# A four-layer graph network on one core: FFN chunks of 4, 4, 4, 4, 4, 3, 2, 1 blocks instead of 3, 4, 4, 4, 4, 4, 2, 1, and the last block's V work in one go

## The chip, the cores and the metric

The kernel runs on one core of a Trainium2 chip. The metric is the device time of one execution in microseconds (us), the median of three runs. Before the change it is 2567.61 us (2564.39 to 2570.67).

## The reference

There are 3327 nodes with 256 features and a sparse 0/1 adjacency matrix. Layer 0 is a simple graph attention over the neighbours. Layers 1 to 3 are transformer layers whose attention is masked by the same adjacency; each of them computes

```
q, k, v = split(layer_norm(x) @ w_qkv)          # 8 heads of 32
attn    = softmax(where(adj != 0, q·k * SCALE, -inf))
x       = x + (attn · v) @ w_proj + b_proj
x       = x + gelu(layer_norm(x) @ w1 + b1) @ w2 + b2     # 256 -> 1024 -> 256
```

About 16 of the 3327 entries of an adjacency row are set, so attention is a weighted sum over a short list of neighbours.

## The kernel before, in words

Layer 0 reads the whole adjacency matrix, makes a list of neighbours for each node and sorts the nodes by degree into 26 blocks of 128 (`NB`). Block 0 holds the nodes with most neighbours: `CAPS` says how many list entries each block has, from 40 for block 0 and 24 for block 1 down to 10 for block 25. The K and V rows of all nodes lie in a DRAM table `kv[L]`, one for each of the layers 1 to 3.

Layers 1 to 3 go through the blocks in the hand-written `ORDER` 25, 1, 24, 2, 23, 3, ... 10, 15, 11, 14, 12, 13, 0 (L1268): long and short ones take turns, and the longest, block 0, comes last. The lists are cut into groups of at most four entries (`slots`, L1275): 121 groups in a layer, ten of them for block 0. `issue` (L1288) fetches a group: for each of its entries GpSimd (POOL) starts one indirect DMA that brings 128 rows of K and V, 2 KB each, into one of the ten buffers (`NBUF`) of a ring. A buffer is free for the next group when the V work of its group is done.

`run` (L1556) writes the order of everything by hand; each engine executes its own instructions in that order. One turn of its inner loop takes one group g of block b:

- `scores` (here called K work): VectorE (DVE) multiplies K by q (L1325) and sums over the head dimension (L1326); after the last group `softmax` follows (L1331, exp on ScalarE, ACT).
- `value`, called once or twice in a turn (L1577), takes the oldest group of an earlier block whose scores are done (`todo`): `values` (V work) multiplies V by the weights on DVE (L1366), sums over entries by transposing matmuls on TensorE (PE, L1372), and issues the next group of gathers (L1375). In a turn of block 0 it is always called twice.
- `some` (L1544) emits pieces of what comes later. `short` holds the five steps of a finished block (`block`: copy, projection on PE, residual add on DVE, L1400). `long` holds the steps of an FFN chunk. Each turn adds `rate` to a credit, and steps with a cost in a made-up unit are taken from `long` while the credit is above zero.

An FFN chunk is made of several finished blocks[...]. When the last block of a chunk has had its residual add, `chunk` (L1411) appends its steps to `long`: normalisation (`scale2`, `turn`, `hT`), eight `up` and eight `down` matmul pairs with a GELU on ACT between them (L1439, L1445, L1462), the way back to rows (`shift`, `back`), the residual adds, and, in layers 1 and 2, the normalisation, Q, K, V (L1492) of the next layer and the store of the new K and V rows (`keep`, L1498 to L1500). In layer 3 the output rows are stored by POOL instead (`store`, L1505). All of a chunk's steps depend on each other in a row across DVE, ACT and PE.

The next layer's gathers may touch any row, so they begin only when the last chunk's K and V rows have been stored: between two layers POOL has nothing to do.

What the change touches:

- the sizes of the chunks (L1270): 3, 4, 4, 4, 4, 4, 2, 1, in the order of `ORDER`. The last ones are 10, 15, 11, 14 (here C10/4, called by its first block and its size), 12, 13 (C12/2) and 0 (C0/1); the one before is C8/4.
- the pace (L1405 to L1407): the sum of the costs in `long`, divided by the number of groups of the next four blocks less two, and by five for the chunk that ends with block 13.
- how often `value` is called (L1577), and the loop after the last group (L1583), in which each `value` is followed by `some`, so that FFN steps are mixed into the V work of block 0.

Of the kernel before, what the change touches and what calls it, by code (L numbers as in the profile page):

```python
# [32 lines left out]
NB = (N + P - 1) // P  # L33
# [25 lines left out]
NBUF = 10  # L59

CB = 4
# [447 lines left out]
@with_exitstack  # L509
def kernel(ctx: ExitStack, tc: tile.TileContext, ins, out: bass.AP):  # L510
    nc = tc.nc
    keep = ctx.enter_context(tc.tile_pool(name="s_keep", bufs=1))
    dram = ctx.enter_context(tc.tile_pool(name="s_dram", bufs=1, space=DRAM))
    flag = keep.tile([1, 1], I32, name="flag")
    E = mybir.EngineType
    with tc.manual_schedule(engines={E.PE, E.DVE, E.Activation, E.Pool, E.SP}):
        with ExitStack() as inner:
            sparse_path(inner, tc, ins, out, dram, flag)
    unfit = nc.values_load(flag[0:1, 0:1])
    with tc.If(unfit > 0):  # L520
        general_path(tc, ins, out)


def sparse_path(ctx, tc, ins, out, dram, flag):
# [98 lines left out]
    with tc.tile_pool(name="a", bufs=1) as a, tc.tile_pool(name="aw", bufs=2) as aw, \  # L623
# [462 lines left out]
        for g in reversed(range(NG)):  # L1086
            at = dict(zip(names, (0, 1, 3, 4, 5, 6, 7, 8, 9, 10, 11, 12)))
# [179 lines left out]

    ORDER = [b for k in range(NB // 2) for b in (NB - 1 - k, k + 1)][:NB - 1] + [0]  # L1268
    CHUNK, at = {}, 0
    for n in [CB - 1] + [CB] * ((NB - CB - 2) // CB) + [2, 1]:  # L1270
        for b in ORDER[at:at + n]:
            CHUNK[b] = ORDER[at:at + n]
        at += n
    assert at == NB
    slots = {b: [(b, s) for s in range(0, CAPS[b], GS)] for b in ORDER}  # L1275

    class Layer:
# [102 lines left out]
        def block(self, b):  # L1380
            L, w, c = self.L, self.w, {}
            x = t2[:, b, :D]
            chunk = CHUNK[b]
            if b == chunk[0]:
                self.n2 = Norm(len(chunk), f"f{L}_{b}")
            n2 = self.n2

            def copy_T():
                c["oT"] = work.tile([P, 2 * P], FP, tag="oT", name=f"oT_{L}_{b}")
                nc.scalar.copy(c["oT"], self.po[b][:, :2 * P])  # L1390

            def project():
                ps = self.po[b][:, D:]
                nc.tensor.matmul(ps, ones_bf[:96, :], bias3[:, 0, :], start=True, stop=False)  # L1394
                for k in range(2):
                    nc.tensor.matmul(ps, c["oT"][:, k * P:(k + 1) * P], w["w_proj"][:, k, :],  # L1396
                                     start=False, stop=(k == 1))

            def add():
                nc.vector.tensor_add(x, x, self.po.pop(b)[:, D:])  # L1400
                n2.stats(chunk.index(b), x)
                if b == chunk[-1]:
                    self.long += self.chunk(chunk, n2)
                    at = ORDER.index(b) + 1
                    turns = sum(len(slots[i]) for i in ORDER[at:at + CB])  # L1405
                    turns = 5 if at == NB - 1 else turns - 2
                    self.rate = sum(cost for cost, _ in self.long) / max(turns, 1)  # L1407

            return [lambda: None, copy_T, project, lambda: None, add]
# [146 lines left out]
        def run(self):  # L1556
            for _ in range(NBUF):
                self.issue()
            self.take_q(ORDER[0])

            todo, wait = [], {}

            def value():
                if todo[0][1] == 0:
                    self.weights(todo[0][0])
                self.values(*todo.pop(0))

            for k, b in enumerate(ORDER):
                for g in slots[b]:
                    self.scores(*g)  # L1570
                    if g == slots[b][-1]:
                        self.softmax(b)
                        if k + 1 < NB:
                            self.take_q(ORDER[k + 1])
                    for i in wait:
                        wait[i] += 1
                    for _ in range(2 if len(todo) > NBUF // 2 or b == 0 else 1):  # L1577
                        if todo and wait[todo[0][0]] > 1:
                            value()
                    self.some()  # L1580
                todo += slots[b]
                wait[b] = 0
            while todo:  # L1583
                value()
                self.some()
            self.rate = 4.0
            while self.short or self.long:
                self.some()
# [45 lines left out]
```

## Time and profile before

The profiled execution took 3156.3 us, 589 us more than the median of the timed ones, so its durations of single instructions can be used, and its sums over long stretches only with care.

| | us | share of the span |
|---|---|---|
| DVE busy | 1935.3 | 61% |
| PE busy | 1794.0 | 57% |
| POOL busy | 1362.7 | 43% |
| ACT busy | 774.6 | 25% |
| granted PE clock, mean | 0.735 | |
| layer 0 (to the first gather) | 509.5 | 16% |
| layer 1 (first gather to first gather of layer 2) | 919.0 | 29% |
| layer 2 | 877.3 | 28% |
| layer 3 (to the end) | 850.5 | 27% |

In a row of a timeline the columns are the start (us from the start of the span), the duration, the engine, the line of the kernel, the instruction, what it writes and reads, how many of them, and in brackets for how long the engine had been idle before and what released it. A busy POOL row is the generation of one gather's descriptors; the data come later.

### The profile page before, as it was taken

The page shows a single profiled execution, that of the slowest core. Times are in us where ns is not written, and L with a number is a line of the kernel's source. Part 1 is how long each engine was busy: PE and PEld are TensorE (multiplying, and loading weights), DVE is VectorE, ACT ScalarE, POOL GpSimd, SP SyncE. Part 2 cuts the span into 40 slices and gives each one's busy share as a digit, 9 for nine tenths or more (in the row PEclk, how much of TensorE's full clock was granted, in tenths as well). Part 3 has the DMA queues.
Part 4 walks back from the last instruction along what each step waited for, and adds up shares of the span by engine and source line. Part 5 has one row for each costly group of instructions (what it writes and reads, how often), then busy time and mean ns, then how long its engine had stood idle before and what let it go on. Part 6 is the DMA issues. An engine that isn't in the chain of part 4 may idle for free.

```text
span 3156.3 us, 24036 instructions
## 1 busy us (share of the span) xinstructions
PE 1794.0 (57%) x7561; PEld 1163.5 (37%) x7561; DVE 1935.3 (61%) x3983; ACT 774.6 (25%) x1316; POOL 1362.7 (43%) x1458
## 2 busy tenths in 40 slices
PE   4767752255666666671457667666713435665556
PEld 3645531133333333350334333433512323433334
DVE  6688995457657656533656756755446556656554
ACT  4455621012222222230112212222300111212112
POOL 4000004545555554305555555544054555565550
PEclk9868766577787886785578778878755766776768
DMA  5334306645555565415455555555064554554560
GB/s 207 131 117 148 129 31 204 174 138 169 165 172 162 156 174 152 112 51 177 141 156 156 163 160 150 175 152 140 24 189 125 156 155 135 169 163 147 161 156 13
DMA packets 144486, 453.80 MB, mean 144 GB/s; under 512 B 29521, under 2 KB 40156, under 8 KB 141021
## 3 DMA queue, kind: packets, MB, share of 16 engines
q0 software_dynamic: 113056, 370.26, 40.9%
q1 hardware_dynamic: 9834, 53.90, 4.9%
q10 hardware_dynamic: 21458, 28.02, 2.5%
q8 instruction: 61, 1.00, 0.1%
q14 instruction: 77, 0.63, 0.1%
HBM read 420.64 MB, written 31.42 MB: 143 GB/s over the span
## 4 chain that ended last, share of the span: by engine, by line
DVE 25%; issue 18%; PE 18%; another core or an unknown queue 17%; POOL 11%; ACT 5%; DMA 5%; DVEq 0%; ACTq 0%; POOLq 0%; SPq 0%
POOL kv L1303 11%; DVE kv L1325 5%; DMA kv<-kv,t 4%; DVE sc L1326 3%; DVE vw L1366 3%; PE pu L1439 3%; PE po L1372 3%; PE py L1462 2%; DVE cand L735 2%; PE pk L1492 1%; PE s_pk L1010 1%; ACT s_aT L724 1%; DVE s_v L731 1%; PE pf L591 1%
## 5 line engine op out<-in xcount | busy, mean ns | idle before, releaser
L1303 POOL DMA_INDIRECT kv<-kv,t x1344 | 1273.0, 947 | 1210.3 <-issue 534.2
L1372 PE MATMUL po<-s_ident,vw 128*128 128x128 f32 x2688 | 475.4, 334 | 580.2 <-DVE vw L1366 387.2
L1372 PEld LDWEIGHTS po<-s_ident,vw 128*128 128x128 f32 x2688 | 395.5, 174 | 724.1 <-issue 373.5
L1325 DVE TENSOR_TENSOR kv<-kv,q 128x1024 f32<-128x1024 f32 (+3 forms) x363 | 413.1, 1138 | 397.1 <-ACT q L1311 274.6
L1366 DVE TENSOR_TENSOR vw<-kv,w 128x1024 f32<-128x1024 f32 x333 | 371.4, 1128 | 87.2 <-remote 84.6
L1326 DVE TENSOR_REDUCE sc<-kv 128x32 f32<-128x1024 f32 (+3 forms) x363 | 414.1, 1141 | 12.4
L1439 PE MATMUL pu<-fT,s_w 128*128 128x512 f32 (+3 forms) x768 | 341.2, 579 | 62.3 <-issue 35.8
L1462 PE MATMUL py<-gT,s_w 128*128 128x512 f32 (+2 forms) x672 | 321.8, 597 | 58.1 <-issue 50.2
L1400 DVE TENSOR_TENSOR t<-t,po 128x256 f32<-128x256 f32 x78 | 32.6, 418 | 390.8 <-remote 254.5
L1445 ACT ACTIVATE gT<-pu,pvb 128x512 f32<-128x512 f32 (+3 forms) x192 | 115.7, 607 | 628.2 <-remote 384.1
L1439 PEld LDWEIGHTS pu<-fT,s_w 128*128 128x128 f32 x768 | 157.4, 222 | 196.1 <-issue 146.4
L1462 PEld LDWEIGHTS py<-gT,s_w 128*128 128x128 f32 x672 | 132.6, 206 | 180.7 <-issue 144.0
L1396 PEld LDWEIGHTS po<-s_w_proj,oT 128*128 128x128 f32 x312 | 71.8, 255 | 281.8 <-issue 272.3
L1394 PE MATMUL po<-bias,s_ones_bf 96*128 96x256 bf16 x78 | 25.2, 324 | 259.7 <-issue 147.4
L1390 ACT COPY oT<-po 128x256 f32<-128x256 f32 x78 | 28.9, 371 | 548.5 <-remote 320.2
L711 POOL MEMSET s_abf<- 128x1 bf16 x23 | 2.2, 104 | 361.4 <-DVE s_v L731 253.7
L1492 PE MATMUL pk<-s_w_qkv,nT 128*128 128x512 f32 x208 | 128.4, 748 | 22.0 <-ACT nT L596 9.9
L735 DVE MAX8 cand<-s_v 128x8 f32<-128x208 bf16 x416 | 118.0, 360 | 0.9
L1396 PE MATMUL po<-s_w_proj,oT 128*128 128x256 f32 x312 | 113.1, 500 | 0.0
L723 PE MATMUL s_ptb<-s_ident_bf,s_abf 128*128 128x128 bf16 x676 | 67.1, 265 | 68.3 <-ACT s_abf L714 45.2
L591 PE MATMUL pf<-s_ident,xn_f 128*128 128x128 f32 x156 | 46.1, 444 | 86.8 <-ACT xn_f L588 66.7
L855 PE MATMUL s_pa<-s_aT,s_hs 128*128 128x256 bf16 x338 | 82.3, 290 | 13.2 <-DVE s_hs L817 13.2
(288 smaller groups left out, 2252.1 us busy)
## 6 DMA issues: line engine op xcount, KB each, us to landing
s_a<-in_adj_dram SPq DMA_DIRECT2D x25, 1663.5 KB
kv<-kv,t POOLq DMA_INDIRECT x1344
kv<-kvr ACTq DMA_DIRECT2D x52, 256.0 KB
kv<-s_kvr ACTq DMA_DIRECT2D x26, 256.0 KB
s_w<-in_L_gnn_w_dram SPq DMA_DIRECT2D x6, 1024.0 KB
t<-ql ACTq DMA_DIRECT2D x6, 592.0 KB
t<-s_x ACTq DMA_DIRECT2D x6, 512.0 KB
s_w_qkv<-in_L_gnn_w_qkv_dram SPq DMA_DIRECT2D x3, 768.0 KB
```

The costliest lines, as they stand in the source:

```text
L735: nc.vector.max(out=self.cand[:, s, :], in_=self.v[:, s, :])
L855: nc.tensor.matmul(self.pa[:, c0:c0 + 2 * P], S.hs[:r, k, :P], aT[:r, k, :], start=(k == 0), stop=(k == NB - 1))
L1303: nc.gpsimd.indirect_dma_start(out=t[:, s, :], out_offset=None, in_=kv[L], in_offset=bass.IndirectOffsetOnAxis(ap=t2[:, b, k:k + 1].bitcas ...
L1325: nc.vector.tensor_mul(k, k, self.q[b][:, None, :].to_broadcast([P, n, D]))
L1326: nc.vector.tensor_reduce(self.sc[b][:, s0:s0 + n, :], k.rearrange("p s (h d) -> p s h d", d=HD), AX.X, ALU.add)
L1366: nc.vector.tensor_mul(vw[:, :n * D].rearrange("p (s h d) -> p s h d", h=HEADS, d=HD), v, self.wp[b][:, s0:s0 + n, :, None].to_broadcast([ ...
L1372: nc.tensor.matmul(self.po[b][:, k * P:(k + 1) * P], vw[:, at:at + P], ident, is_transpose=True, start=(s0 + s == 0 and k == 0), stop=(s0 ...
L1396: nc.tensor.matmul(ps, c["oT"][:, k * P:(k + 1) * P], w["w_proj"][:, k, :], start=False, stop=(k == 1))
L1439: nc.tensor.matmul(c["pu", f][:, :n], w["w1"][:, e, f * P:(f + 1) * P], c["hT"][:, e, :n], start=(e == 0), stop=(e == 1))
L1445: nc.scalar.activation(g[:, :n], c.pop(("pu", f))[:, :n], AF.Gelu_apprx_tanh, bias=w["b1"][:, f:f + 1])
L1462: nc.tensor.matmul(c["py"][e][:, :n], w["w2"][:, f, e * P:(e + 1) * P], g[:, :n], start=(f == 0), stop=last)
L1492: nc.tensor.matmul(ps[:, :c1 - c0], c["hT"][:, e, j * P:(j + 1) * P], nxt["w_qkv"][:, e, c0:c1], start=(e == 0), stop=(e == 1))
```

## The change

The first chunk gets one block more, the last chunk but two one fewer, so that the sizes are 4, 4, 4, 4, 4, 3, 2, 1. The last chunks are then 17, 9, 16, 10 (C17/4), 15, 11, 14 (C15/3), 12, 13 (C12/2) and 0 (C0/1). It is meant to leave less FFN work for the time after the last gather. Each chunk is spread over the groups of the blocks of the next chunk, less two, instead of over the next four blocks: for C17/4 these are 11 turns, for C15/3 seven, for C12/2 eight. In a turn of block 0 `value` is called once, as in other turns. After the last group the ten V steps of block 0 are emitted in one go, and what is left of the FFN steps comes behind them.

```diff
@@ -1267,7 +1267,7 @@
-    for n in [CB - 1] + [CB] * ((NB - CB - 2) // CB) + [2, 1]:
+    for n in [CB] * ((NB - 6) // CB) + [3, 2, 1]:
         for b in ORDER[at:at + n]:
             CHUNK[b] = ORDER[at:at + n]
@@ -1402,8 +1402,7 @@
                     at = ORDER.index(b) + 1
-                    turns = sum(len(slots[i]) for i in ORDER[at:at + CB])
-                    turns = 5 if at == NB - 1 else turns - 2
+                    turns = sum(len(slots[i]) for i in CHUNK[ORDER[min(at, NB - 1)]]) - 2
                     self.rate = sum(cost for cost, _ in self.long) / max(turns, 1)
@@ -1574,7 +1573,7 @@
-                    for _ in range(2 if len(todo) > NBUF // 2 or b == 0 else 1):
+                    for _ in range(2 if len(todo) > NBUF // 2 else 1):
                         if todo and wait[todo[0][0]] > 1:
                             value()
@@ -1582,7 +1581,6 @@
             while todo:
                 value()
-                self.some()
             self.rate = 4.0
             while self.short or self.long:
                 self.some()
```

## The prediction

> **What bounds the kernel now.** I first read the groups of the page, for the one instruction that sets the pace of layers 1 to 3, and then POOL's timeline at the end of layer 1.
>
> ```profile
> L1303 POOL DMA_INDIRECT kv<-kv,t x1344 | 1273.0, 947 | 1210.3 <-issue 534.2
> ...
> 1309.57 0.95 POOL L1303 DMA_INDIRECT kv<-kv,t  x1 [0.30 <-issue]
> 1310.82 0.95 POOL L1303 DMA_INDIRECT kv<-kv,t  x1 [0.30 <-issue]
> 1428.53 1.44 POOL L1303 DMA_INDIRECT kv<-kv,t  x1 [116.76 <-DVE s_part L1255]
> ```
>
> A gather costs POOL 0.95 + 0.30 = 1.25 us even with nothing to wait for. A layer has 448 of them (1344 / 3): 560 us, and a full group of four takes 5.0 us. The last two rows are the hole between layers: 117 us without a gather (114 in layer 2; in layer 3, 87 us from the last gather to the end). Layer 0 (509.5) + 3 x 560 + 52 more indirect DMAs (65) + these tails (317) = 2572, against 2567.6 measured. So the timed kernel is close to POOL's pace plus three tails; the profiled one is stretched by waits like this, from ACT's timeline:
>
> ```profile
> 1273.50 0.69 ACT L1445 ACTIVATE gT<-pu,pvb 128x512 f32<-128x512 f32 x1 [7.18 <-remote]
> ...
> 1309.72 0.69 ACT L1445 ACTIVATE gT<-pu,pvb 128x512 f32<-128x512 f32 x1 [21.98 <-remote]
> ...
> 1316.11 0.37 ACT L1390 COPY oT<-po 128x256 f32<-128x256 f32 x1 [5.62 <-remote]
> ```
>
> They stand only where gathers run, and I take them out below. Next, DVE's and ACT's timelines, for the length of a chunk's chain:
>
> ```profile
> 1255.91 0.17 DVE L551 TENSOR_SCALAR rqv_f<-mv_f 128x4 f32<-128x4 f32 x1
> 1333.60 0.17 DVE L551 TENSOR_SCALAR rqv_n<-mv_n 128x4 f32<-128x4 f32 x1
> ...
> 1353.75 0.33 ACTq L1500 DMA_DIRECT2D kv<-kvr  x1
> 1354.47 1.28 ACT L1340 ACT_TABLE_LOAD   x1
> 1402.85 0.60 ACT L588 ACTIVATE xn_f<-t,nm_f,rqy_f 128x256 f32<-128x256 f32 x1 [4.93 <-DVE nm_f L582]
> 1422.91 0.39 ACTq L1500 DMA_DIRECT2D kv<-kvr  x1
> ```
>
> C10/4 runs from 1255.9 to 1354.1: 98 us, of which PE lost some 23 to the three waits above, so 75 to 76. Only then can ACT, which works in order, do the exp of block 0. From there to the first gather of layer 2 it is 1428.5 - 1354.1 = 74.4 us (C12/2 with half of block 0's V work, the other half, the projection, C0/1 with 25.7 from its xn_f). This half has no odd waits, so I use it as it stands (layer 2: 73.9).
>
> The bound at the end of a layer is therefore the FFN chain, not POOL: the last gather is generated at 1311.8, and its data could be used some 4 us later.
>
> **What the skill says.** The Trainium skill, "TensorE: Matmul & The Clock Gate" (Part 1: The HAM clock gate) has PE's clock halved until it has been busy for about 3.4 us. The trace agrees: after a pause of PE the first four K/V matmul pieces of a chunk took 3.78 us, later ones 1.72; each restart of a chain pays about 2 us. "ScalarE: Activation LUTs" (What ACT_TABLE_LOAD costs) gives 1.28 us for a table load, as the row above shows, so an exp among GELUs costs two. "DMA: Bandwidth & Descriptors" says that the descriptors of GpSimd's DMAs are written by software there; it gives no price for this shape, the trace does (1.25).
>
> **The change part by part.** No instruction that matters is added or removed; only the first and one later chunk change size. I lay the chains end to end, with turns at POOL's pace.
>
> *Lengths.* C10/4 by sums: scale2 2.6; turn and hT 3.9; 8 x (1.72 up + 1.72 down) = 27.5 and 3.8 for the cold start; nine V groups at 0.87 on PE and two projections at 1.3, which lie between = 10.4; shift and back 2.2; adds, scale1 and a K group between = 9.2; turn and hT 3.9; Q, K, V and keep 14.0. Together 77.5, against 75 to 76 from the trace: I use 76. For three blocks: up and down 8 x 2.58 = 20.6 and 3.8; six V groups and one projection 6.5; the adds come in one turn, so 5.4; Q, K, V 11.4; the rest 12.4: 60. C17/4 in 11 turns has fewer V groups between its steps: 73.
>
> *Before, from the point where C8/4 is queued (group 90).* C10/4 is queued at group 108, which is 65 gathers later = 81 us at POOL's pace; C8/4 (76) is done by then. 81 + 76 + 74.4 = **231**.
>
> *After, from the same point.* C17/4 is queued when block 10 is done, at group 95: 19 gathers = 24 us. It has 11 turns, in which POOL needs 46 us, but its chain needs 73. The residual adds of the chunk and of block 11 stand in DVE's order, so DVE waits for the chain: at 24 + 73 = 97 the chunk is done. Three more turns of K and V work, about 7 us of DVE, lead to the add of block 14, which queues C15/3 at 104, not at POOL's 81. C15/3 takes 60: 164. Behind it come block 13's copy, projection and add, 2.8, and C12/2.
>
> *The tail after.* From C12/2's scale2: 2.6 and 2.3 to the first up; up and down to the seventh GELU about 12; then the exp of block 0, which stands behind that GELU in ACT's order, with its load, 1.9; weights 1.7; ten V groups on DVE at 1.22 = 12.2, PE's last 1.0. Only then, by the order written, C12/2 goes on: back, two adds, scale1 5.4; turn and hT 2.7; Q, K, V twice 5.6 and keep 0.5; C0/1 25.7. Sum 73.6, and with the 2.8, **76.4**. The old order has 74.4 here. Taking `some` out of the loop costs about 2 us: before, five of the ten V groups lay beside C12/2's chain, now DVE's 12 us lie on the path with PE and ACT nearly idle. Total: 164 + 76.4 = **240**, 9 us more for each of layers 1 and 2.
>
> *POOL.* With one `value` a turn the last issue comes in the fifth turn of block 0, not the third. About four groups are ahead (20 us), so at an even pace this is free. When DVE waits for C15/3's adds, the next V work, and with it the next gather, waits too: about 10 us of POOL's time. It is hidden, since the last K group is still done before the seventh GELU.
>
> *Layer 3* has no Q, K, V in a chunk and the chain is 24 us shorter; POOL is the bound there. Before, from group 108: 60 for POOL, then C12/2 with V0 37.7 and C0/1 to the end 26.9 (rqv_f at 3091.7, 3129.4, end 3156.3): 125. After: C15/3's three stores stand among the last gathers on POOL, about 3 us each; C12/2's head ends by 77, then exp 2, weights 2, V0 13, adds 3, and C0/1 27: 124 to 126. I put +1.
>
> Sum: 2 x 9 + 1 = +19: **2587 us**. At the start of a layer the first chunk waits six turns (24 gathers, 30 us) longer; at POOL's pace that is not on the path. If the chains already lag behind POOL in the timed kernel, it is, and each layer loses 4 to 6 us more.
>
> **The rivals.** (1) *Faster: the chain fits.* If C17/4's steps, emitted closer, need no more than about 57 us (POOL's from group 95 to 108), C15/3 starts at 81 and ends at 141, and the total is 217: 14 us less for each of two layers, and the layer 3 tail a few us less: about 2540. For it: PE's own share of a chunk is about 45 us, and the smaller chunk leaves less after the last gather, where PE is under full use (81% granted clock, 66% busy). Against it: the sum of durations, which already is without gaps. (2) *Slower by more: chains lag.* If the waits marked "remote" also stand in timed runs, the chains are the pace throughout, the late start of the first chunk and DVE's waits at the adds come on top, with POOL running dry: 15 us or more in each of two layers, 5 in the third, about 2603 to 2615. For it: in the trace 4-chunks come every 114 to 124 us, far from POOL's 83. (3) *No change:* the C15/3 that is shorter by 16 us and the late start of it cancel; 2563 to 2572.
>
> **How the numbers follow.** My forecast (a few us to 1% slower) has 0.42; rival 2 has 0.21; no change 0.11; faster 0.26. So faster 0.26, same 0.11, slower 0.63. The range takes in the chain's length (70 to 80 us: +8 to +36 in all) and, since the faster case is above 2 in 10, part of that: 2548 to 2616.
>
> **What would show it.** In the trace after: C17/4 from rqv_f (four blocks, fifth of its kind) to its last store in over 65 us beside odd waits; a C15/3 that starts late; DVE waiting at L1480 and L1400 inside block 12 and the first groups of block 0; POOL waiting for V work there; ten V groups in a row with no FFN matmul between them, then back (L1476); 74 to 78 us from C15/3's last store to the next gather. I am wrong if the hole between the last gather and the next layer shrinks by more than POOL is held up before it, for instance if C15/3 starts right at group 108.

## The result and the profile after

| | median, us | lowest to highest | ratio to before, with its 95% interval |
|---|---|---|---|
| before | 2566.99 | 2564.39 to 2570.67 | |
| after | 2602.64 | 2599.51 to 2606.41 | 1.0138 [1.012, 1.0157] |

The change makes the kernel 35.6 us slower; 2587 was forecast, with a range of 2548 to 2616. The timed runs of before, at 2564 to 2571 us, can't have had the long waits that stretched its first profile to 3156 us, and the profile of after has none. So everything below is compared with a second profile of before, of 2566.9 us (experiment 0).

First the page after: the span, the granted PE clock, and the group of the gathers (busy, mean ns, then the idle time ahead of them).

```profile
span 2600.3 us, 24028 instructions
PEclk8767876656987788787568897888865778868778
L1303 POOL DMA_INDIRECT kv<-kv,t x1344 | 1274.1, 948 | 673.9 <-issue 346.3
```

The same of before, from its second profile:

```profile
span 2566.9 us, 24036 instructions
PEclk9778777657788788887577889788865876877888
L1303 POOL DMA_INDIRECT kv<-kv,t x1344 | 1273.0, 947 | 643.8 <-issue 321.6
```

The gathers cost what they did, 1274 us; POOL waits 30 us more. The mean granted clock is 0.771 after and 0.784 before, but PE's matmuls are no slower for it (an `up` matmul takes 552 ns on the mean, 551 before, with the same sizes in another order), so the clock is not what costs the 35 us. Where POOL waits has changed far more than that sum says. POOL's timeline of the kernel after, end of layer 2:

```profile
1725.25 0.94 POOL L1303 DMA_INDIRECT kv<-kv,t  x1 [4.51 <-DVE vw L1366]
...
1749.92 0.94 POOL L1303 DMA_INDIRECT kv<-kv,t  x1 [9.77 <-DVE vw L1366]
...
1759.61 0.94 POOL L1303 DMA_INDIRECT kv<-kv,t  x1 [3.75 <-DVE vw L1366]
...
1827.57 0.94 POOL L1303 DMA_INDIRECT kv<-kv,t  x1 [9.40 <-DVE vw L1366]
...
1841.33 0.95 POOL L1303 DMA_INDIRECT kv<-kv,t  x1 [0.31 <-issue]
1919.92 0.94 POOL L1303 DMA_INDIRECT kv<-kv,t  x1 [77.65 <-DVE s_row L1259]
```

And the end of layer 2 before, which began its layer at 1200.92 (after: 1217.09):

```profile
1704.65 0.94 POOL L1303 DMA_INDIRECT kv<-kv,t  x1 [2.68 <-DVE vw L1366]
1712.44 0.94 POOL L1303 DMA_INDIRECT kv<-kv,t  x1 [3.10 <-DVE vw L1366]
...
1788.63 0.94 POOL L1303 DMA_INDIRECT kv<-kv,t  x1 [0.30 <-issue]
1887.11 0.94 POOL L1303 DMA_INDIRECT kv<-kv,t  x1 [97.53 <-DVE s_row L1259]
```

The hole between the layers did shrink, as the change means it to: 97.53 to 77.65 us. But the last gather of the layer starts 1841.33 - 1217.09 = 624.2 us after the first, against 587.7 before: 36.5 us later. 36.53 - 19.88 = 16.65, which is the whole loss of layer 2. That is bookkeeping and not yet a cause. Of the 36.5, 7.6 have gathered when C17/4 is queued. The rest is in sight: from there on seven holes of over 2 us sum to 37.2 (four of them are shown; the others are 3.55, 3.02 and 3.19), where before has two of 5.8 in all. Each ends with V work on DVE (L1366), which frees a buffer.

DVE's timeline after tells why. The rows with `rqv_f` mark the start of C17/4, C15/3, C12/2 and C0/1 (columns of sizes x4, x3, x2, x1); the adds (L1479, which is L1480 before) stand near the end of a chunk.

```profile
1703.02 0.21 DVE L551 TENSOR_SCALAR rqv_f<-mv_f 128x4 f32<-128x4 f32 x1
...
1743.94 0.42 DVE L1479 TENSOR_TENSOR t<-t,pd 128x256 f32<-128x256 f32 x1 [9.91 <-PE pd L1475]
...
1783.65 0.17 DVE L551 TENSOR_SCALAR rqv_f<-mv_f 128x3 f32<-128x3 f32 x1
...
1818.03 0.42 DVE L1479 TENSOR_TENSOR t<-t,pd 128x256 f32<-128x256 f32 x1 [9.92 <-PE pd L1475]
...
1844.65 0.17 DVE L551 TENSOR_SCALAR rqv_f<-mv_f 128x2 f32<-128x2 f32 x1
...
1853.24 1.22 DVE L1326 TENSOR_REDUCE sc<-kv 128x32 f32<-128x1024 f32 x1
...
1864.53 0.73 DVE L1346 TENSOR_REDUCE den<-sc 128x8 f32<-128x320 f32 x1 [9.54 <-ACT sc L1340]
...
1866.06 11.44 DVE L1366 TENSOR_TENSOR vw<-kv,sc 128x1024 f32<-128x1024 f32 x10
...
1885.19 0.15 DVE L551 TENSOR_SCALAR rqv_f<-mv_f 128x1 f32<-128x1 f32 x1
```

Before, in the same place, C8/4, C10/4, and the exp's consumer after them:

```profile
1652.24 0.17 DVE L551 TENSOR_SCALAR rqv_f<-mv_f 128x4 f32<-128x4 f32 x1
...
1741.00 0.17 DVE L551 TENSOR_SCALAR rqv_f<-mv_f 128x4 f32<-128x4 f32 x1
...
1787.33 0.42 DVE L1480 TENSOR_TENSOR t<-t,pd 128x256 f32<-128x256 f32 x1 [2.83 <-PE pd L1476]
...
1815.49 0.73 DVE L1346 TENSOR_REDUCE den<-sc 128x8 f32<-128x320 f32 x1 [8.78 <-ACT sc L1340]
```

At the adds of C17/4 DVE stands for 9.91 us and POOL, one V step later, for 9.77; the same pair comes with C15/3 (9.92 and 9.40). Before, the wait at the adds of C10/4 was 2.83. The row at 1853.24 is the end of the last K group of block 0. The ten V groups of block 0 are one row of 11.44 us. ACT's timeline after shows what the exp of block 0 stands behind:

```profile
1862.15 0.47 ACT L1444 ACTIVATE gT<-pu,pvb 128x256 f32<-128x256 f32 x1 [1.25 <-PE pu L1438]
1862.64 1.28 ACT L1340 ACT_TABLE_LOAD   x1
1863.94 0.56 ACT L1340 ACTIVATE sc<-sc,mx 128x320 f32<-128x320 f32 x1
```

The table load takes 1.28 us, the figure of the Trainium skill, "ScalarE: Activation LUTs" (What ACT_TABLE_LOAD costs). The same section adds a drain of about 1.38 us for every switch. These rows show none: the load starts 0.02 us after the GELU ends, and the exp 0.02 us after the load.

By layer, in us, from first gather to first gather (layer 3: to the end). Layer 1 is counted here from POOL's first fetch of a block's own rows, 5 us ahead of its first gather of K and V. Differences are taken before rounding:

| | layer 1 | layer 2 | layer 3 |
|---|---|---|---|
| before | 702.1 | 686.2 | 679.8 |
| after | 715.6 | 702.8 | 680.4 |
| difference | +13.5 | +16.7 | +0.6 |

The three sum to 30.8; the remaining 2.6 of the traces' 33.4 lie in layer 0, which the change does not touch and whose length differs by more than that between the profiles of experiments 0 to 7 (497.2 to 501.7).

### The profile page after: what moved, and what is told of

Read it like the earlier page. It is cut to its first block, busy times and chain, and to the rows that moved or that the text cites. A ratio compares the mean times of both kernels' runs of the same rounds, so it can differ in the third digit from the quotient of the medians.

```text
span 2600.3 us, 24028 instructions
## 1 busy us (share of the span) xinstructions
PE 1695.0 (65%) x7561; PEld 1140.2 (44%) x7561; DVE 1937.5 (75%) x3983; ACT 778.2 (30%) x1316; POOL 1363.9 (52%) x1458
## 5 line engine op out<-in xcount | busy, mean ns | idle before, releaser
L1303 POOL DMA_INDIRECT kv<-kv,t x1344 | 1274.1, 948 | 673.9 <-issue 346.3
L1372 PE MATMUL po<-s_ident,vw 128*128 128x128 f32 x2688 | 464.4, 332 | 526.9 <-DVE vw L1366 525.4
L1372 PEld LDWEIGHTS po<-s_ident,vw 128*128 128x128 f32 x2688 | 390.1, 172 | 648.2 <-DVE vw L1366 546.4
L1366 DVE TENSOR_TENSOR vw<-kv,w 128x1024 f32<-128x1024 f32 x333 | 371.8, 1128 | 1.7
L1438 PE MATMUL pu<-fT,s_w 128*128 128x512 f32 (+3 forms) x768 | 320.1, 552 | 12.8 <-ACT gT L1444 10.3
L1461 PE MATMUL py<-gT,s_w 128*128 128x512 f32 (+2 forms) x672 | 283.6, 549 | 1.8 <-ACT gT L1444 1.8
L1461 PEld LDWEIGHTS py<-gT,s_w 128*128 128x128 f32 x672 | 124.4, 192 | 103.2 <-issue 81.6
L1491 PE MATMUL pk<-s_w_qkv,nT 128*128 128x512 f32 x208 | 117.6, 694 | 8.0 <-ACT nT L596 8.0
L588 ACT ACTIVATE xn_f<-t,nm_f,rqy_f 128x256 f32<-128x256 f32 x78 | 43.1, 594 | 225.1 <-DVE nm_f L582 219.0
L1396 PE MATMUL po<-s_w_proj,oT 128*128 128x256 f32 x312 | 105.2, 471 | 0.0
L1340 ACT ACTIVATE sc<-sc,mx 128x120 f32<-128x120 f32 (+6 forms) x78 | 32.0, 410 | 230.6 <-DVE mx L1337 230.0
L723 PEld LDWEIGHTS <-s_abf 128*128 128x128 bf16 x676 | 57.7, 124 | 78.2 <-ACT s_abf L714 55.9
L855 PE MATMUL s_pa<-s_aT,s_hs 128*128 128x256 bf16 x338 | 81.9, 289 | 13.2 <-DVE s_hs L817 13.2
```

Of the source, the lines that this page charges most:

```text
L723: nc.tensor.transpose(pt[:, m, :], self.abf[:, k * P:(k + 1) * P], ident_bf)
L1303: nc.gpsimd.indirect_dma_start(out=t[:, s, :], out_offset=None, in_=kv[L], in_offset=bass.IndirectOffsetOnAxis(ap=t2[:, b, k:k + 1].bitcas ...
L1366: nc.vector.tensor_mul(vw[:, :n * D].rearrange("p (s h d) -> p s h d", h=HEADS, d=HD), v, self.wp[b][:, s0:s0 + n, :, None].to_broadcast([ ...
L1372: nc.tensor.matmul(self.po[b][:, k * P:(k + 1) * P], vw[:, at:at + P], ident, is_transpose=True, start=(s0 + s == 0 and k == 0), stop=(s0 ...
L1438: nc.tensor.matmul(c["pu", f][:, :n], w["w1"][:, e, f * P:(f + 1) * P], c["hT"][:, e, :n], start=(e == 0), stop=(e == 1))
L1461: nc.tensor.matmul(c["py"][e][:, :n], w["w2"][:, f, e * P:(e + 1) * P], g[:, :n], start=(f == 0), stop=last)
```

## The experiments

In the expectations the theories have letters: A is the prediction's own account (sizes and pace), B puts the loss on the two other parts (one `value` a turn, V work in one go); A1 and A2 part the sizes from the pace, and D concerns the copy of q, told at its place. "Sizes" is the line L1270, "pace" the lines of `turns`, "one value" the edit in the turns of block 0, "one go" the `some` taken out of the last loop. Experiments 0 to 3 share one set of runs of before (median 2572.06), 4 to 7 another (2568.99), 8 to 11 a third.

**0. The kernel before, unchanged.** No edit; a second profile.

> The kernel before, unchanged, for a trace without the long waits of the first one. Theory A (the compressed chains C17/4 and C15/3 make DVE wait at their adds, so that V work and the gathers behind it come late): POOL is held up by less than 10 us between group 90 and the last gather of a layer, where the trace of the kernel after shows some 30 to 37 us, and the hole from the last gather to the next layer's first is 85 to 95 us, longer than the 77.6 us after. Theory B (the order of the tail: V of block 0 in one go): POOL is held up about as after, and the hole is 10 to 12 us shorter than after, about 66 us. Span about 2567 us.

One execution took 2568.74 us, the profile 2566.9. It has no wait marked "remote". The holes on POOL at the end of layer 2 are 2.68 and 3.10 us, the hole between layers is 97.5. C8/4's last store is out at 1731.4, 9.6 us before C10/4 is queued (1741.00). So in an undisturbed execution the FFN chains keep up with POOL at the end of a layer, and the chains of the last chunks alone set the hole.

**1. Sizes and pace without the other two parts.**

```diff
-    for n in [CB - 1] + [CB] * ((NB - CB - 2) // CB) + [2, 1]:
+    for n in [CB] * ((NB - 6) // CB) + [3, 2, 1]:
...
-                    turns = sum(len(slots[i]) for i in ORDER[at:at + CB])
-                    turns = 5 if at == NB - 1 else turns - 2
+                    turns = sum(len(slots[i]) for i in CHUNK[ORDER[min(at, NB - 1)]]) - 2
```

> Only the chunk sizes and the pace of the kernel after; two V groups a turn in block 0 and FFN steps between its V groups after the last K group, as before. Theory A: nearly the whole loss, 2592 to 2603 us. Theory B: no loss, 2562 to 2572 us.

2604.62 us, ratio 1.0127 [1.011, 1.0144]: as slow as the whole change. Layers 721.9, 710.1 and 671.3: layers 1 and 2 lose 20 and 24, layer 3 gains 8.5. The loss is all here; B falls.

**2. One go alone.**

```diff
             while todo:
                 value()
-                self.some()
```

> The kernel before, and only the FFN steps between the V groups of block 0 after the last K group are taken out. Theory A: 0 to 3 us a layer, 2567 to 2576 us. Theory B: most of the loss, 2590 to 2603 us.

2562.35 us, ratio 0.9963 [0.9949, 0.9978]: faster than before by 10 us, which neither theory had. Layers 701.7, 686.2 and 673.9: nothing in layers 1 and 2, 6 us in layer 3 (what else the two profiles differ by, 2 us, lies in layer 0). DVE's timeline before, end of layer 3, shows what was in the way (the adds of C12/2, then V work of block 0, then the start of C0/1):

```profile
2526.03 0.75 DVE L1480 TENSOR_TENSOR t<-t,pd 128x256 f32<-128x256 f32 x2 [11.81 <-PE pd L1476]
2526.69 9.23 DVE L1366 TENSOR_TENSOR vw<-kv,sc 128x1024 f32<-128x1024 f32 x8
...
2539.91 0.15 DVE L551 TENSOR_SCALAR rqv_f<-mv_f 128x1 f32<-128x1 f32 x1
```

and with one go alone:

```profile
2517.20 8.04 DVE L1366 TENSOR_TENSOR vw<-kv,sc 128x1024 f32<-128x1024 f32 x7 [4.82 <-PE po L1372]
...
2531.97 0.75 DVE L1480 TENSOR_TENSOR t<-t,pd 128x256 f32<-128x256 f32 x2 [0.81 <-PE pd L1476]
2532.64 0.15 DVE L551 TENSOR_SCALAR rqv_f<-mv_f 128x1 f32<-128x1 f32 x1
```

Mixed in, C12/2's adds make DVE wait 11.81 us with eight V groups behind them, and C0/1 needs those eight. In one go the V groups fill that wait. C12/2 (started at 2497.15 before, at 2493.89 here) to C0/1 takes 38.75 us instead of 42.76: 4 of the 6. In layer 2 the same happens, C10/4 to C0/1 takes 109.1 instead of 117.8, but from C0/1 to the next gather it is then 36.6 instead of 28.3, and nothing is left of the gain. C12/2 still has its Q, K and V to do there: its last store comes at 1858.06, behind the start of C0/1 (1848.45), while before it came at 1850.46, ahead of that start (1858.82).

**3. One value alone.**

```diff
-                    for _ in range(2 if len(todo) > NBUF // 2 or b == 0 else 1):
+                    for _ in range(2 if len(todo) > NBUF // 2 else 1):
```

> The kernel before, and only the second V group in the turns of block 0 is taken out, so that the last gathers are issued up to two turns later. Theory A: nothing by itself, since four groups are ahead, 2564 to 2571 us. A theory C (the later issue starves POOL): 5 us or more in each layer, 2580 us and more.

2568.72 us, ratio 0.9987 [0.998, 0.9994]: nothing to speak of. Layers 698.5, 682.8 and 683.7: it gains 3.6 and 3.4 and gives back 3.9.

**4. The kernel after, with q copied earlier.** This tests the late start of the chunks. In the kernel after DVE's waits for the copy of the next block's q (ACT, L1311) have grown, by the list of waits after (engine, line, releaser: us in all, times, longest):

```profile
DVE kv L1325 <- ACT q L1311: 145.3, 43, 7.9
```

and before:

```profile
DVE kv L1325 <- ACT q L1311: 100.2, 38, 7.3
```

(With the sizes alone, experiment 6, it is 119.5.)

That copy is emitted behind the softmax of the block, and so stands in ACT's order behind whatever FFN work came with that turn. Here it is emitted in the first turn of the block before it.

```diff
                     self.scores(*g)
+                    if g == slots[b][0] and k + 1 < NB:
+                        self.take_q(ORDER[k + 1])
                     if g == slots[b][-1]:
                         self.softmax(b)
-                        if k + 1 < NB:
-                            self.take_q(ORDER[k + 1])
```

> The kernel after, and the copy of the next block's q (L1311) is emitted in the first turn of a block instead of behind the exp that ends it, so that DVE never waits for it behind GELUs of a chunk. Theory D (the late start of C17/4 comes from DVE waiting for q on ACT: 145 us in all in the trace after, 100 us before): the chunk queue times of layers 1 and 2 move forward by 6 us and more, and the total falls to 2575 to 2592 us. Theory E (it comes from POOL and the ring alone, DVE's waits for q only stand in for waits for gathers): 2598 to 2605 us.

2587.59 us, ratio 1.0071 [1.0054, 1.0088]: by the ratio about half of the loss comes back, by the layers of the profile a third, 10 us of 30.8. The wait falls to 79.8 us. The start of C17/4 in layer 2, whose first gather is at 1210.76 here:

```profile
1688.38 0.17 DVE L551 TENSOR_SCALAR rqv_f<-mv_f 128x4 f32<-128x4 f32 x1
```

That is 477.6 us after the layer's first gather instead of 485.9 (1703.02 - 1217.09). The layer takes 696.7, 6.1 less; layer 1 takes 711.8, 3.8 less; layer 3 is unchanged at 680.4. So the copy of q is what made the chunks late in the kernel after. The 8.3 us are not won in full, as the close pace is still there: the hole on POOL at C15/3's adds is now 13.2 us.

**5. Early q and one go in the kernel before.** The edits of 4 and 2 in the old sizes and pace.

> The kernel before with its old chunk sizes, the copy of q in the first turn of a block, and no FFN steps between the V groups of block 0 after the last K group. Theory D: less to gain than in the kernel after, since DVE waits less for q there: 2540 to 2558 us. Theory E: as without the early copy, 2559 to 2566 us.

2563.95 us, ratio 0.9984 [0.9975, 0.9994], against 0.9963 [0.9949, 0.9978] with one go alone: the early q brings nothing there, though DVE's wait for it falls from 99.0 to 65.6 us. Layers 701.6, 686.3 and 674.2 are those of 2. The expected gain missed: in the old sizes this wait costs nothing, so it lies beside something longer; what that is, no run shows.

**6. Sizes alone.** The first pair of lines of 1, with the old `turns`.

> The kernel before with the new chunk sizes alone; the pace is the old one, so C17/4 is spread over 16 turns, not 11, and C15/3 over 17, not 7. Theory A1 (the compressed pace, which makes DVE wait at the adds, is the loss): 2570 to 2590 us. Theory A2 (the chains one after another are the loss, whatever the pace; a slower pace only makes them longer): 2602 to 2625 us.

2579.55 us, ratio 1.0043 [1.0027, 1.006]. Layers 705.4, 693.0 and 679.8. A2, by which only the chains' sum counts and the pace does not, falls; A1 holds. The end of C17/4 in DVE's timeline, layer 2, with sizes alone:

```profile
1690.25 0.18 DVE L551 TENSOR_SCALAR rqv_f<-mv_f 128x4 f32<-128x4 f32 x1
...
1733.96 0.42 DVE L1400 TENSOR_TENSOR t<-t,po 128x256 f32<-128x256 f32 x1 [0.94 <-PE po L1396]
1734.97 0.39 DVE L1480 TENSOR_TENSOR t<-t,pd 128x256 f32<-128x256 f32 x1
...
1763.98 0.34 DVE L551 TENSOR_SCALAR rqv_f<-mv_f 128x3 f32<-128x3 f32 x1
```

DVE reaches C17/4's adds (L1480) without a wait where it stood 9.91 us after: the steps are spread over 16 turns instead of 11, so their inputs are there when their turn comes, and K and V work fills the time. (At C15/3's adds it still waits, 6.81 us instead of 9.92.) C15/3 starts 73.7 us after C17/4, not 80.6. The last store of C17/4, first here and then in the kernel after, shows where the difference lies:

```profile
1764.60 0.33 ACTq L1500 DMA_DIRECT2D kv<-kvr  x1
...
1774.46 0.33 ACTq L1499 DMA_DIRECT2D kv<-kvr  x1
```

C17/4 itself takes 74.7 us here and 71.8 after, so the close pace hardly shortens it. But here the next chunk starts 1.0 us before that store is out, and after 8.9 us behind it: K and V work that lay beside the chain comes on top of it.

**7. Two smaller chunks at the end.** The kernel after with early q and other sizes.

```diff
-    for n in [CB] * ((NB - 6) // CB) + [3, 2, 1]:
+    for n in [3, 4, 4, 4, 4, 3, 2, 2]:
```

> The kernel after with the early copy of q and chunks of 3, 4, 4, 4, 4, 3, 2, 2 blocks: the first chunk starts as early as before, and what remains behind block 0 is a chunk of two, not of one. Theory A2 with D: the chains start 30 us earlier and the last three have 3, 2, 2 blocks: from the sums about 675 us for layer 2, 2545 to 2560 us in all. If the early start is worth nothing: as e4 or slower.

2587.79 us, ratio 1.0082 [1.0063, 1.0101]; layers 705.1, 692.0 and 686.6. The hoped-for gain missed. In layer 2 the chunks come at 81, 62 and 56 us, and the last needs 42: 241 from the place where C8/4 is queued, against 245 in 4, and layer 3 is 6.3 longer than in 4. The close pace still leaves holes of 12.5, 10.9 and 10.0 us on POOL.

**8 to 11. The old pace, and mixtures by layer.** 8 is the kernel after with the old `turns`. The other three choose by layer: layer 3 with the new sizes and pace, which had given 671 us there in 1, and its old loops; layers 1 and 2 with the old pace and

- 9: the old sizes, and one go
- 10: the sizes of 7, with `some` left in the last loop
- 11: the sizes of 7, and one go

```diff
-    for n in [CB - 1] + [CB] * ((NB - CB - 2) // CB) + [2, 1]:
...
+    CHUNKS = {L: chunks([3, 4, 4, 4, 4, 3, 2, 2] if L < LAYERS[-1] else [4, 4, 4, 4, 4, 3, 2, 1]) for L in LAYERS}
...
                     turns = 5 if at == NB - 1 else turns - 2
+                    if nxt is None:
+                        turns = sum(len(slots[i]) for i in CHUNKS[L][ORDER[min(at, NB - 1)]]) - 2
```

(`chunks` is the old loop made a function; 9 has the old sizes in the first list; 9 and 11 have `if self.nxt is None:` ahead of `self.some()` in the last loop.)

What was expected of 8:

> The kernel after with the pace of the kernel before (chunks spread over the next four blocks, less two turns). Theory A1 (the compressed pace makes DVE wait at the adds of C17/4 and C15/3, and the K and V work held up there comes on top of the chains): the holes of POOL at those chunks go, C15/3 follows C17/4 after 73 to 75 us instead of 80.6, layers 1 and 2 become about 10 us shorter each, 2572 to 2585 us. Theory A2 (only the sum of the chains counts): 2598 to 2606 us.

Of 9 (here called e9):

> Layers 1 and 2 as in the kernel before, without FFN steps between the last V groups; layer 3 with the sizes and the pace of the kernel after, but two V groups a turn in block 0 and FFN steps between the last V groups, as layer 3 was in e1 (671 us there, 680 before). If a layer's time follows its own order alone: 2554 to 2561 us. If it doesn't: about 2567 us.

Of 10:

> As e9, but layers 1 and 2 with chunks of 3, 4, 4, 4, 4, 3, 2, 2 at the old pace and FFN steps between the last V groups. Theory A1 with chains that follow each other without DVE waiting at adds: 58 for C10/3 from 526 us after the layer's start, about 43 for C14/2 beside V0, 42 for the last chunk: 675 us for layer 2 instead of 686, in all 2532 to 2550 us. If the chains still make DVE wait: 2557 to 2575 us.

Of 11:

> As e10, with the V groups of block 0 in one go in layers 1 and 2. If V0 beside the chain of C14/2 is worth something: 2 to 6 us a layer slower than e10. If, as in e2, it makes no difference in layers 1 and 2: the same as e10.

On the chip of these four the kernel before itself took 3149.07 us (26 runs, 3135 to 3170), so only the ratios mean anything, and only for that condition:

| | median, us | ratio to before there |
|---|---|---|
| 8, after with old pace | 3177.61 | 1.0097 [1.0065, 1.0129] |
| 9, layer 3 new, one go | 3171.17 | 1.0076 [1.0049, 1.0103] |
| 10, sizes of 7, old pace | 3162.24 | 1.0063 [1.0035, 1.0091] |
| 11, as 10, one go | 3154.51 | 1.0018 [1.0003, 1.0033] |

None is faster there; the expected times missed. The list of waits of 8 has what the first profile of before has too, waits for something that the trace can't name ("remote"):

```profile
ACT gT L1445 <- remote: 294.1, 23, 30.0
ACT oT L1390 <- remote: 285.8, 18, 26.3
DVE t L1400 <- remote: 245.1, 13, 24.0
```

For their own questions 8 to 11 are inconclusive: whether any of them beats before where before takes 2567 us is open. Of 0 to 7, one go alone (2) has the lowest ratio; it beats both kernels.

## Why the prediction was right, and by how much its terms were off

The direction held and the mechanism mostly; the size was half. The parts, from traces 0, 6, 1 and after, layer by layer, in us:

| | layer 1 | layer 2 | layer 3 |
|---|---|---|---|
| sizes (6 less before) | +3.3 | +6.9 | -0.1 |
| pace on top (1 less 6) | +16.5 | +17.0 | -8.5 |
| one value and one go on top (after less 1) | -6.3 | -7.3 | +9.1 |
| sum | +13.5 | +16.7 | +0.6 |
| predicted | +9 | +9 | +1 |

**The working in layer 2, term by term**, the terms of before from the profile of 0, those of after from the rows shown:

| term | predicted | measured |
|---|---|---|
| before: C8/4 to C10/4 | 81 | 88.8 |
| before: C10/4's chain | 76 | 72.6 |
| before: from there to the next gather | 74.4 | 73.5 |
| before, sum | 231 | 234.9 |
| after: C8/4 point to C17/4 | 24 | 34.6 |
| after: C17/4's chain | 73 | 71.8 |
| after: three turns to C15/3 | 7 | 8.9 |
| after: C15/3's chain | 60 | 58.1 |
| after: to C12/2 | 2.8 | 2.85 |
| after: tail from C12/2 | 73.6 | 75.3 |
| after, sum | 240 | 251.5 |

(The C8/4 point is the place in a layer at which C8/4 is queued before, 451.3 us after the layer's first gather; C17/4 is queued at 485.9 after.)

- *The mis-sized term* is the first one after: "19 gathers = 24 us", with "at POOL's pace that is not on the path" of the late start of the first chunk. It measured 34.6 (31.4 in layer 1), 10.6 too much, and is the largest of the errors in a sum that missed by 11.5. Part of it is pace: even before, block 10's add came 478.2 - 451.3 = 26.9 us behind that point, not 24, and the first term of before was 7.8 too small as well. Errors of that kind are in both sums; what the difference of the two missed by is 7.6 (16.6 measured, 9 forecast), and most of that is the late start: after, the same add comes at 484.8, 6.6 later. The prediction had named a loss of about that size, "each layer loses 4 to 6 us more", but for the case that the chains already lag behind POOL in the timed kernel. They don't (experiment 0), so the size came right by luck: the late start stands in executions without any odd wait, and with the sizes alone (in 6 C17/4 is queued at 485.9 too). Experiment 4 names the carrier: with q copied early, C17/4 is queued 26.3 us behind the point (477.6), and the late start is gone. It wasn't the length of a chain but one small copy in ACT's order, which the prediction never looked at. Why it bites in the new sizes and not in the old ones (experiment 5) is argued only: a chunk now begins behind other, shorter blocks.
- *"At POOL's pace" was too fast, and the check of it came out by luck.* The prediction's sum for the whole kernel before, 2572 against 2567.6 measured, rests on two errors that cancel. In the undisturbed profile the three layers take 1800 us from the start of the first gather to the end of the last, where 1745 were reckoned (3 x 560 and 65), and the three tails are 96.6, 97.5 and 68.8 us, together 263, not 317.
- *DVE waits for C17/4's adds, so C15/3 starts late and not at group 108*: right, and shown. The chain is 71.8 long, the wait 9.91 us, and the spread over few turns is the cause: with the old pace (6) the wait is gone and C15/3 follows after 73.7. The pace is by far the dearest part of the change in layers 1 and 2. The prediction didn't price it by itself; with it the chunks lie end to end, as its sum has them, and without it they overlap.
- *POOL is held up by about 10 us, hidden*: the size was too small, the rest right. The holes grew by 31.4 us (37.2 less 5.8) in layer 2. It had counted the adds of C15/3 alone (9.40), not those of C17/4 (9.77) nor the five short ones. Even so POOL is not what the end of the layer waits for: the last K group is done at 1854.46, and the exp behind it has to stand behind the seventh GELU until 1862.6.
- *The tail after*: right in each point (exp behind the seventh GELU, ten V groups in a row, C12/2 only then), 75.3 against 73.6.
- *Taking `some` out costs about 2 us*: wrong. It costs nothing in layers 1 and 2 and gains 6 in layer 3 (2). With one value, in the new sizes, layers 1 and 2 even gain 6 and 7. The prediction had five V groups lying beside C12/2's chain in the old order; in layer 2 of before DVE does three, then stands for 15.92 us at C12/2's adds (1836.43) with the other seven behind them.
- *One `value` a turn is free for POOL*: right in the old sizes (3), where it costs layer 3 alone 3.9 us. In the new sizes the last gather of layer 3 comes 622.9 us after its first, with the old two values 611.1 (1). POOL's timeline shows why. After, the three output stores of C15/3 (L1504) stand ahead of the last four gathers, 11.9 us from the first store to the next gather:

```profile
2527.04 1.00 POOL L1504 DMA_INDIRECT out_dram<-t,perm  x1 [0.30 <-issue]
2534.51 1.00 POOL L1504 DMA_INDIRECT out_dram<-t,perm  x1 [6.47 <-DMA out_dram<-t,perm]
2537.70 0.97 POOL L1504 DMA_INDIRECT out_dram<-t,perm  x1 [2.19 <-issue]
2538.97 0.98 POOL L1303 DMA_INDIRECT kv<-kv,t  x1 [0.30 <-issue]
...
2542.77 0.95 POOL L1303 DMA_INDIRECT kv<-kv,t  x1 [0.30 <-issue]
```

With sizes and pace alone (1) they come behind the last gather (layer 3 starts at 1930.67 there, at 1919.92 after):

```profile
2541.79 0.94 POOL L1303 DMA_INDIRECT kv<-kv,t  x1 [0.30 <-DMA kv<-kv,t]
2543.03 0.99 POOL L1504 DMA_INDIRECT out_dram<-t,perm  x1 [0.30 <-issue]
```

- *Layer 3, +1*: +0.6 measured, in part by luck. The stores among the last gathers were foreseen, at about 9 us. But both sums were too short by about the same, which cancels: from the place where C10/4 is queued before, 129.1 us before and 129.6 after, against 125 and 124 to 126. And the parts are large: sizes and pace gain 8.5 there, since C12/2 starts 8.6 us sooner with the new pace (602.6 against 611.2 in 6, from the layer's start) and POOL's last gather is at 611 in both; the other two parts give it back. That it is the one value which puts the stores ahead of the last gathers follows from the order written, as the last loop begins only after the last gather is issued; in the new sizes it wasn't run by itself.

The rival "faster" needed C15/3 to start at group 108; it started 80.6 us behind C17/4. The rival "slower by more" (2603 to 2615) came out at its lower edge, nearer than the forecast, and with half of its reasons: POOL runs dry and the late start counts, but not because of waits marked "remote", of which no undisturbed trace has one.

## What to carry to other kernels

A step whose input comes from a chain should be emitted no sooner than the chain can be ready: spread over fewer turns than its own length in time, an FFN chunk hardly gets faster (71.8 us against 74.7), its adds stop the engine on which the other work is queued (9.9 us on DVE, and 9.8 on POOL behind it), and that work then comes on top of the chain. When a hole after the last transfer shrinks, look first at how far that last transfer itself has moved: here 20 us were won and 36 lost. And before a late start is called free, follow the smallest operation that the next stage needs through its engine's order; here it was a copy on ACT. Whether it costs anything has to be tried: in the old sizes the same copy moved forward brought nothing (5).

## What the runs showed of the hardware beyond that

The same unchanged kernel took 2567 to 2572 us in three sets of runs and 3149 in a fourth, on another chip, with all 26 executions within 3135 to 3170. The longer executions come with waits that the trace calls "remote" on ACT, DVE and PE, of up to 42 us each and, but for one of 0.6 us, only while gathers run; the profiles of 0 to 7 and of after have none. No run here shows what causes them. No kernel but before was run in both conditions, so it is open how far the ratios of one hold in the other.
